# Layer 0's block attention with queries and outputs in seven block products each, beside each other in banks of their own and in a written-out order

## The chip, the cores and the metric

The kernel runs on one core of a Trainium2 chip. The time is device microseconds of one execution, the lower the better. TensorE is called PE here (its weight loads PEld), VectorE DVE, ScalarE ACT, GpSimd POOL, and SyncE, which issues the DMAs, SP.

## The reference, cut to what matters

Two decoder layers on x of 8 sequences by 112 tokens by 512 channels (896 tokens), all in float32. Each layer has a self-attention, a cross-attention to a context and a third block. In Layer 0 the third block is a decoder block of its own: a grouped-query attention with 32 query heads and 4 key-value heads of 128 channels, and then a mixture of 32 experts. The change is in that attention:

```python
h = _rmsnorm(hidden_states, ln1_w)
q = (h @ Wq).reshape(B, S, 32, 128)      # Wq: 512 x 4096
k = (h @ Wk).reshape(B, S, 4, 128)       # Wk, Wv: 512 x 512
v = (h @ Wv).reshape(B, S, 4, 128)
q, k = _rope(q, pos), _rope(k, pos)
k, v = jnp.repeat(k, 8, axis=2), jnp.repeat(v, 8, axis=2)
scores = jnp.einsum('bqhd,bkhd->bhqk', q, k) / jnp.sqrt(128.0)
scores = jnp.where(causal, scores, -1e9)
attn = jax.nn.softmax(scores, axis=-1)
o = jnp.einsum('bhqk,bkhd->bqhd', attn, v).reshape(B, S, 4096) @ Wo   # Wo: 4096 x 512
x = resid + o
```

The experts that follow read x, and the residual path needs the x from before as well.

## The kernel before

**Layout.** Activations stand either with tokens on partitions (x and y, seven tiles of 128 tokens by 512 channels) or transposed with channels on partitions (hT: four chunks of 128 channels by 896 tokens). HALF is 448 tokens, half of all. The eight PSUM banks of 128 x 512 float32 are named by hand: bank 0 and 1 for projections (`mm_ps`), 2 and 3 for scores (`sc_ps`), 4 and 5 for transposes (`tp_ps`), 6 and 7 for averages (`o_ps`), each pair used in turn.

**The attention** (`l0_block_attention`). The 32 query heads go in eight head groups, hg, of four heads; two groups share one key-value head. First come the keys of all heads and the queries of group 0 (`project_T`, 128 channels by 448 tokens at a time, four matmuls each; `rope_halves` turns each with one DVE multiplication, two DVE multiplications of 64 partitions and one POOL addition), then the values. Then, for each group, a loop over the eight sequences b; one turn of it is called a step here. A step holds:

- `probabilities`: four score matmuls of 112 x 112, on DVE the scale and mask, the row maximum and its subtraction, the exponential on ACT, on DVE the row sum and its reciprocal, on POOL the division;
- `project_queries`: one block of the next group's queries, 128 channels by 448 tokens (32 matmuls a group; an fp32 matmul is two PE records, so 64), and its rope;
- `average`, two steps late: four transposes of the probabilities, a copy to SBUF by ACT, one matmul with the values, a copy to oT by ACT;
- `project_out`, LAG = 5 tiles late: one tile of 128 tokens of oT times Wo's part of the group, four matmuls of 512 columns, and an addition to y by DVE;
- `gather_weights`: DMAs that bring one part of the experts' weights from one place in DRAM to another, which wait for a value of this step so that they are spread over the stage.

The weights of a group, wq and wo, are loaded into a pool of six tiles (`load_w`). The stage isn't ordered by hand: the framework's scheduler sets the order of the instructions on each engine by its own costs. Other stages put `with in_order():` around their work, which keeps each engine to the order in which the code issues.

**Seven products.** Layer 1's FFN already multiplies matrices in two by two blocks with seven block products where eight are usual, by `seven_products`. Sums and differences of blocks stand in for the blocks: `row_sums` makes four of the stationary side, `column_sums` four of the moving side. Partial results stay in three PSUM banks a, b, c: a collects a first product, is copied by ACT, collects the next on top, is copied again, and so on; `take` adds a copy to a bank and stores the block:

```python
product(a, top[0], left[0], first=True);  m1 = copied(0)
product(c, rows[0], columns[0], first=True)
product(a, rows[1], columns[1]);          u2 = copied(1)
product(b, top[1], left[1], first=True)
product(a, rows[2], columns[2]);          u3 = copied(2)
take(1, 1, c, u3);  take(0, 0, b, m1)
product(a, bottom[1], columns[3]);        take(1, 0, a, None)
product(c, rows[3], right[1]);            take(0, 1, c, u2)
```

In the trace before, L259 is the projections' matmul, L888 scores, L304 transposes, L913 averages, L841, L844 and L848 the rope, L904 the division, L306 and L917 ACT's copies, L922 the addition to y, L1410 the matmul of the seven products, L1387 to L1390 the row sums and L1394 to L1397 the column sums. L80 is the line of an engine wrapper, which every instruction inside `in_order` has.

Of the kernel before, what the change touches and what calls it, by code (L numbers as in the profile page):

```python
# [21 lines left out]
FP = mybir.dt.float32  # L22
# [36 lines left out]
def decoder(ctx: ExitStack, tc: tile.TileContext, a, out: bass.AP):  # L59
# [756 lines left out]

    def block_norm(y, t, root):

        mvr = row_scales(x[t], root, (ONCE, twice(1e-5)))
        yield  # L820
        xn = normed_rows()
        normed(xn, x[t], mvr, mvr[:, 3:4])
        shift = sm.tile([P, 1], FP, tag="shift", name="shift", bufs=8)
        V.tensor_scalar(shift, mvr[:, 0:1], mvr[:, 2:3], -1.0, ALU.mult, ALU.mult)
        A.activation(y[t], x[t], AF.Identity, bias=shift, scale=mvr[:, 2:3])
        return xn
# [23 lines left out]
    def l0_block_attention(y, hT, late, weights, prepare):  # L850
# [5 lines left out]

        wk_, wv = load_w(a["f0_wk"], "f0_wk"), load_w(a["f0_wv"], "f0_wv")
        with phase("f0", "tile") as p0:
            kT = p0.tile([P, 4, NT], FP, tag="kT", name="kT")
# [10 lines left out]
            v = p0.tile([S, B, D], FP, tag="v", name="v")  # L870
            for half in range(2):
                for g in range(4):
                    rope_halves(kT[:, g, half * HALF : (half + 1) * HALF], project_T(hT, wk_, g, half))
                for j in range(4):
                    project_queries(qT, wq, 4 * half + j)
                if half == 0:
                    for xn, t in late:
                        transpose_tile(hT, xn, t, ln1w)
            for b in range(B):
                pp = mm_ps()  # L880
                matmul_k(pp[:S, :], lambda k: hT[:, k, b * S : (b + 1) * S], lambda k: wv[:, k, :])
                A.copy(v[:, b, :], pp[:S, :])

            def probabilities(hg, qT, b):
                sc = sc_ps()
                tok = slice(b * S, (b + 1) * S)
                for j in range(4):
                    T.matmul(  # L888
                        sc[:S, j * S : (j + 1) * S], qT[:, j, tok], kT[:, hg // 2, tok],
                        start=True, stop=True,  # L890
                    )
                s = work[0].tile([S, 4, S], FP, tag="s", name="s", bufs=4)
                V.scalar_tensor_tensor(
                    s, sc[:S, : 4 * S].rearrange("p (j q) -> p j q", j=4),
                    128.0**-0.5, causal4, ALU.mult, ALU.add,
                )
                mx = sm.tile([S, 4], FP, tag="mx", name="mx")
                V.tensor_reduce(mx, s, AX.X, ALU.max)
                softmax_exp(s, mx)
                den = sm.tile([S, 4], FP, tag="den", name="den")  # L900
                V.tensor_reduce(den, s, AX.X, ALU.add)
# [3 lines left out]
                return s  # L905

            outs = o_ps()

            def average(hg, oT, b, s):
                pT = transpose_probs(s, "pT")  # L910
                po = outs[b % 2]
                kv = hg // 2
                T.matmul(  # L913
                    po[:, : 4 * S], v[:, b, kv * P : (kv + 1) * P],
                    pT.rearrange("p j q -> p (j q)"), start=True, stop=True,
                )
# [4 lines left out]
            def project_out(oT, wo, t):  # L921
                V.tensor_tensor(y[t], y[t], project_rows(oT, wo, t), ALU.add)  # L922

            halves = [a[n].rearrange("e p k n -> (e p) (k n)") for n in ("e0_wg", "e0_wu", "e0_wd")]

            def gather_weights(step, s):

                r = slice(step * P // 2, (step + 1) * P // 2)
                nc.sync.dma_start(weights[step * P // 2 : step * P // 2 + 1, :: KC * NI], s[:1, 0, :3])
                for i, src in enumerate(halves):  # L930
                    nc.sync.dma_start(weights[r, i * KC * NI : (i + 1) * KC * NI], src[r, :])

            waiting, finished = [], []
            for hg in range(8):
                wo = load_w(a["f0_wo"][hg], "f0_wo")
                oT = p0.tile([P, 4, NT], FP, tag="oT", name="oT", bufs=2)
                if hg < 7:
                    qT_next, wq = new_queries(hg + 1)
                else:
                    prepare()  # L940
                for b in range(B):
                    waiting.append((hg, oT, b, probabilities(hg, qT, b)))
                    gather_weights(hg * B + b, waiting[-1][3])
                    if hg < 7:
                        project_queries(qT_next, wq, b)
                    if len(waiting) > 2:
                        average(*waiting.pop(0))

                    if b < NTT:
                        finished.append((oT, wo, b))  # L950
                    if len(finished) > LAG:
                        project_out(*finished.pop(0))
                qT = qT_next
            for one in waiting:
                average(*one)
            for one in finished:
                project_out(*one)
# [424 lines left out]


    def row_sums(dst, top, bottom, eng):


        eng.tensor_tensor(dst(0), bottom[0], bottom[1], ALU.add)  # L1387
        eng.tensor_tensor(dst(1), dst(0), top[0], ALU.subtract)
        eng.tensor_tensor(dst(2), top[0], bottom[0], ALU.subtract)
        eng.tensor_tensor(dst(3), top[1], dst(1), ALU.subtract)  # L1390

    def column_sums(dst, left, right, eng):

        eng.tensor_tensor(dst(0), right[0], left[0], ALU.subtract)  # L1394
        eng.tensor_tensor(dst(1), right[1], dst(0), ALU.subtract)
# [753 lines left out]
```

## Time and profile before

| | |
|---|---|
| median of three runs | 2036.97 us (2033.36 to 2041.16) |
| the profiled execution | 2040.25 us, span 2038.4 us |
| granted PE clock, mean | 0.976 |
| PE busy | 1930.7 us, 95% |
| DVE, ACT, POOL busy | 956.7, 589.5, 723.2 us |
| mean DMA rate | 103 GB/s |

A group line of the profile reads: line, engine, operation, output and inputs by the program's names, shapes, count, then total busy time and the mean length of one in ns, then the idle time before them and what ended it. Lengths of matmuls overlap, since PE is pipelined, so the distance from one start to the next is what one costs.

### The profile page before, as it was taken

To read this page: it belongs to the slowest core of one execution; us is meant where nothing else is said; L and a number is where in the kernel's file an instruction comes from. 1 tells how busy PE (TensorE), PEld (TensorE's weight loads), DVE (VectorE), ACT (ScalarE), POOL (GpSimd) and SP (SyncE) were. 2 spreads that over 40 slices of the span, in tenths; PEclk is the share of its full clock that TensorE was granted. 3 is DMA by queue.
4 is the path that set the end of the run, shared out by engine and by line. 5 is a ranking of instruction groups with operands and counts; after the bars stand their busy time and mean duration, and the time that the engine had idled before them with its cause. 6 is when DMAs were issued, how large, how long until landed. Compare 5 with 4: busy or idle time off the path is not lost. (4 is left out here: it accounts for less than half of the span.)

```text
span 2038.4 us, 26870 instructions
## 1 busy us (share of the span) xinstructions
PE 1930.7 (95%) x10113; PEld 1187.9 (58%) x10113; DVE 956.7 (47%) x1983; ACT 589.5 (29%) x1373; POOL 723.2 (35%) x875
## 2 busy tenths in 40 slices
PE   8999998999999999998999999989889898899999
PEld 4545664455555555554778888864555544445568
DVE  4662556375666656645222222214686556522260
ACT  3543321121122212232111111112466636422200
POOL 2253041132222222221456666631354302344371
PEclk9999989999999999989999999999999999999999
DMA  4105010143344343544886776754001120211100
GB/s 177 42 22 173 13 42 32 57 134 129 126 138 138 131 129 104 161 180 156 268 235 128 214 160 152 187 100 125 22 22 34 54 60 22 84 42 42 41 6 31
DMA packets 82024, 209.65 MB, mean 103 GB/s; under 512 B 32979, under 2 KB 38227, under 8 KB 72788
## 3 DMA queue, kind: packets, MB, share of 16 engines
q1 hardware_dynamic: 57588, 134.27, 20.0%
q0 software_dynamic: 24288, 73.47, 14.2%
q8 instruction: 86, 1.41, 0.3%
q14 instruction: 62, 0.51, 0.1%
HBM read 245.31 MB, written 78.76 MB: 159 GB/s over the span
## 5 line engine op out<-in xcount | busy, mean ns | idle before, releaser
L259 PE MATMUL bank<-f_wo,oT 128*128 128x512 f32 x448 | 210.5, 594 | 0.0
L259 PE MATMUL bank<-hT,f_wq 128*128 128x448 f32 x512 | 202.6, 540 | 0.0
L80 PEld LDWEIGHTS bank<-hbT,wb 128*128 128x128 f32 x1408 | 164.2, 192 | 20.6 <-issue 20.6
L904 POOL TENSOR_TENSOR s<-s,rec 112x448 f32<-112x448 f32 x64 | 59.8, 934 | 322.1 <-ACT pT L306 252.2
L80 DVE TENSOR_TENSOR hidb<-sgb,bank 128x256 f32<-128x256 f32 x66 | 27.8, 422 | 291.1 <-ACT sgb L80 229.4
L80 PE MATMUL bank<-hbT,wb 128*128 128x128 f32 x1408 | 164.3, 275 | 0.0
L259 PEld LDWEIGHTS bank<-hT,f_wq 128*128 128x128 f32 x512 | 93.8, 190 | 78.2 <-issue 77.8
L80 POOL TENSOR_TENSOR st<-st,rec 112x448 f32<-112x448 f32 (+1 forms) x95 | 82.9, 904 | 147.7 <-DVE rec L80 83.4
L259 PEld LDWEIGHTS bank<-f_wo,oT 128*128 128x128 f32 x448 | 80.7, 190 | 76.0 <-issue 76.0
L80 POOL DMA_INDIRECT acc<-ob,row_out x66 | 106.3, 1611 | 35.0 <-issue 18.3
L80 ACT ACTIVATE st<-st,mxs 112x112 f32<-112x112 f32 (+1 forms) x383 | 111.0, 379 | 0.0
L298 ACT ACTIVATE s<-s 112x448 f32<-112x448 f32 x64 | 36.9, 577 | 244.0 <-DVE s L297 234.3
L922 DVE TENSOR_TENSOR y<-y,bank 128x512 f32<-128x512 f32 x56 | 38.5, 688 | 124.6 <-PE bank L259 124.6
L848 POOL TENSOR_TENSOR qT<-qT,qs 128x448 f32<-128x448 f32 x64 | 72.4, 1132 | 63.3 <-DVE qs L844 63.3
L844 DVE TENSOR_TENSOR qs<-bank,shape_consts 64x448 f32<-64x448 f32 x144 | 89.5, 622 | 2.9
L80 PE MATMUL bank<-wb,hidb 128*128 128x512 f32 x176 | 84.5, 603 | 0.0
L80 ACT ACTIVATE sgb<-bank 128x256 f32<-128x256 f32 x66 | 25.4, 384 | 202.6 <-PE bank L80 179.0
L80 POOL DMA_INDIRECT hrow<-hrows,row_in x66 | 63.9, 969 | 47.0 <-DVE free L80 23.2
L80 POOL DMA_INDIRECT wb<-weights,wrow x44 | 46.3, 1052 | 95.9 <-PE bank L80 74.1
L1410 PE MATMUL bank<-tok,sums 128*128 128x448 f32 x192 | 78.1, 541 | 2.0 <-DVE tok L1394 1.4
L80 ACT ACTIVATE ob<-bank,pw 128x512 f32<-128x512 f32 x66 | 45.4, 688 | 118.8 <-PE bank L80 117.3
L888 PEld LDWEIGHTS bank<-kT,qT 128*112 128x112 f32 x512 | 59.6, 178 | 27.6 <-issue 25.6
(407 smaller groups left out, 3680.9 us busy)
## 6 DMA issues: line engine op xcount, KB each, us to landing
weights<-in_e_wg SPq DMA_DIRECT2D x64, 256.0 KB
weights<-in_e_wu SPq DMA_DIRECT2D x64, 256.0 KB
weights<-in_e_wd SPq DMA_DIRECT2D x64, 256.0 KB
f_wq<-in_f_wq SPq DMA_DIRECT2D x8, 1024.0 KB
f_wo<-in_f_wo SPq DMA_DIRECT2D x8, 1024.0 KB
cTe<-in_ctxT SPq DMA_DIRECT2D x8, 558.0 KB
f_wg<-in_f_wg SPq DMA_DIRECT2D x4, 1024.0 KB
f_wu<-in_f_wu SPq DMA_DIRECT2D x4, 1024.0 KB
```

The costliest lines, as they stand in the source:

```text
L80: done = issue(*args, **kw)
L259: T.matmul(dst, lhs(k), rhs(k), start=(k == 0), stop=(k == n - 1))
L298: A.activation(s, s, AF.Exp)
L844: V.tensor_tensor(qs[lo : lo + 64], src[hi : hi + 64], sin0[lo : lo + 64].unsqueeze(1).to_broadcast([64, HB, S]), ALU.mult,)
L848: G.tensor_tensor(d, d, qs, ALU.add)
L888: T.matmul(sc[:S, j * S : (j + 1) * S], qT[:, j, tok], kT[:, hg // 2, tok], start=True, stop=True,)
L904: G.tensor_tensor(s, s, rec.unsqueeze(2).to_broadcast([S, 4, S]), ALU.mult)
L922: V.tensor_tensor(y[t], y[t], project_rows(oT, wo, t), ALU.add)
L1410: T.matmul(dst, lhs(k), rhs(k), start=first and k == 0, stop=k == terms - 1, skip_group_check=True)
```

## The change

Queries of groups 1 to 7 and outputs of all groups become seven block products.

- Queries: two products p a group, each two heads by both halves of the tokens, `row_sums` of wq on POOL for each (`qsum`). The token side is summed once for all groups: one sum takes the place of half of hT, three stand in the tiles of x, so x is written to DRAM first (`far_x`) and read back at the end.
- Outputs: tiles of tokens in three pairs, each two tiles by two halves of 256 output channels; `row_sums` of oT on POOL (`osums`), four sums of wo a group on DVE (`osum`). The seventh tile is done as before (`last_output`). Blocks are added to y by DVE from PSUM and by POOL from a copy.
- Banks: bank 5 for scores, bank 6 for transposes and averages, (0, 4, 1) and (7, 4, 1) as a, b, c for queries, (2, 4, 3) for outputs.
- Only two key heads and value heads stay in SBUF; the other two go to DRAM (`far_k`, `far_v`) and come back in groups 2 and 4.
- Softmax: negated scores and a minimum, four exponentials a step on ACT with the minimum as a bias, each of which sums its row itself, for one exponential with a subtraction and a sum on DVE. The division comes one step later. `gather_weights` waits for the row sums.
- The whole stage is `in_order`. Pieces of the products are generators, one piece a block product, in two lists (0: queries, 1: outputs); `fill` runs three times in a step, after the scores, between transposes and average, and after the average, and takes pieces from both lists up to a share of what the group wants. A piece's `row_sums` are issued when it is among the first two of its list and its inputs are there.
- `row_sums`, `column_sums`, `seven_products` and helpers move up in the file; `seven_products` yields after every block product. Layer 1's FFN calls the same functions and keeps its order.

The diff, cut to its core:

```diff
+        product(a, top[0], left[0], first=True)
+        m1 = copied(0)
+        yield
+        product(c, rows[0], columns[0], first=True)
+        yield
+        product(a, rows[1], columns[1])
+        u2 = copied(1)
+        yield
...
+        if terms < 4:
+            take(0, 0, b, m1)
+        yield
...
-            for half in range(2):
-                for g in range(4):
-                    rope_halves(kT[:, g, half * HALF : (half + 1) * HALF], project_T(hT, wk_, g, half))
-                for j in range(4):
-                    project_queries(qT, wq, 4 * half + j)
+            for t in range(NTT):
+                nc.sync.dma_start(far_x[t * P : (t + 1) * P, :], x[t])
+            for g in (3, 2, 1, 0):
+                kT = new_keys()
+                for half in range(2):
+                    rope_halves(kT[:, half * HALF : (half + 1) * HALF], project_T(hT, wk_, g, half))
+                if g < 2:
+                    keys[g] = kT
+                else:
+                    nc.sync.dma_start(far_k[g - 2], kT)
+                project_queries(qT, wq, 7 - g)
...
+            product_banks = [(bank[0], bank[4], bank[1]), (bank[2], bank[4], bank[3]),
+                             (bank[7], bank[4], bank[1])]
+
+            def query_products(qT, wq, p):
+                top, bottom = blocks_of(wq, p)
+                sums = p0.tile([P, 4, 2, P], FP, tag="qsum", name="qsum", bufs=2)
+                row_sums(lambda i: sums[:, i], top, bottom, G)
+                yield
+                copies = [normed_rows()[:, :HALF] for _ in range(3)]
+
+                def take(m, half, pp, more):
+                    if more is not None:
+                        V.tensor_tensor(more, pp, more, ALU.add)
+                        pp = more
+                    later.append((qT[:, 2 * p + m, half * HALF : (half + 1) * HALF], pp))
...
+            def output_products(oT, wo, columns, p, which=1):
...
+                row_sums(lambda i: sums[:, i], top, bottom, G)
+                yield
...
+                def take(m, n, pp, more):
+                    d = y[2 * p + m][:, n * NI : (n + 1) * NI]
+                    V.tensor_tensor(d, d, pp, ALU.add)
+                    if more is not None:
+                        G.tensor_tensor(d, d, more, ALU.add)
...
+            def exps(s, mn):
                 den = sm.tile([S, 4], FP, tag="den", name="den")
-                V.tensor_reduce(den, s, AX.X, ALU.add)
+                for j in range(4):
+                    A.activation(s[:, j, :], s[:, j, :], AF.Exp, bias=mn[:, j : j + 1], scale=-1.0,
+                                 accum_out=den[:, j : j + 1])
+                return s, den
...
+            def fill(share):
+
+                for _ in range(2):
+                    for which in range(2):
+                        if given[which] < share * wanted[which]:
+                            go_on(which)
+                if later:
+                    rope_halves(*later.pop(0))
+
+            waiting, undivided, rest = [], [], None
+            with in_order():
+                for hg in range(8):
...
+                    done = hg * B
+                    given[:] = 0, 0
+                    wanted[:] = 16 * (hg < 7), 25 if hg else 9
+                    if rest:
+                        add(1, output_products(*rest, 1), done - 3)
+                    if hg < 7:
+                        for p in range(2):
+                            add(0, query_products(qT_next, wq, p))
+                    else:
+                        wanted[:] = 16, 13
...
+                    for b in range(B):
...
+                        scores(hg, qT, b)
+                        fill((3 * b + 1) / (3 * B))
+                        s, mn = find_minima()
+                        waiting.append((hg, oT, b, s))
+                        if undivided:
+                            divide(*undivided.pop())
+                        one = waiting.pop(0) if len(waiting) > 2 else None
+                        if one:
+                            pT = turned(one[3])
+                        fill((3 * b + 2) / (3 * B))
+                        if one:
+                            average(*one[:3], pT)
+                            averaged[0] += 1
+                            make_ready()
+                        if b == 4:
+                            columns = output_sums(wo)
+                        if b == 5:
+                            add(int(hg < 7), output_products(oT, wo, columns, 0, int(hg < 7)), done + 3)
+                        undivided.append(exps(s, mn))
+                        gather_weights(hg * B + b, undivided[0][1])
+                        fill((3 * b + 3) / (3 * B))
...
+                divide(*undivided.pop())
+                for one in waiting:
+                    go_on(0)
+                    go_on(1)
+                    average(*one[:3], turned(one[3]))
...
+            for t in range(NTT):
+                nc.sync.dma_start(x[t], far_x[t * P : (t + 1) * P, :])
```

## The prediction

> **What bounds the kernel now.** I read the page first (busy times and the forty slices), then the busy time by stretch, then PE in order of time inside the stage, then the groups by line and shape.
>
> ```profile
> PE 1930.7 (95%) x10113; PEld 1187.9 (58%) x10113; DVE 956.7 (47%) x1983; ACT 589.5 (29%) x1373; POOL 723.2 (35%) x875
> PE   8999998999999999998999999989889898899999
> ```
>
> TensorE bounds the program as a whole. Layer 0's block attention lies in slices 9 to 18. By the view in order of time it runs from the first queries of head group 1 at 406.7 us to the first router transposes at 897.8 us, 491.1 us; PE is busy for 489.65 us of them, at clock 1.00. One head group (8 steps) of it:
>
> ```profile
> core 0: us, PE busy (x) PEld busy (x) DVE busy (x) ACT busy (x) POOL busy (x), PEclk, DMA share, GB/s
> 535.40:599.60 64.20, 64.20 (x233) 34.30 (x232) 39.56 (x71) 13.15 (x24) 16.51 (x16) 1.00 0.40 131
> ```
>
> Nothing waits here but the other engines: DVE has 25 us spare, ACT 51, POOL 48. So PE work taken out shows in full, unless the new order makes PE wait. One step of PE, repeated every 8.47 us:
>
> ```profile
> start us, us, engine line op out<-in xcount [idle before <-releaser]
> 600.60 0.55 PE L304 MATMUL bank<-ident,s 112*112 112x112 f32 x4
> 600.98 1.04 PE L259 MATMUL bank<-f_wo,oT 128*128 128x512 f32 x2
> 601.86 0.98 PE L913 MATMUL bank<-pT,v 112*128 112x448 f32 x2
> 602.68 2.74 PE L259 MATMUL bank<-f_wo,oT 128*128 128x512 f32 x6
> 605.25 0.95 PE L888 MATMUL bank<-kT,qT 128*112 128x112 f32 x8
> 606.04 3.19 PE L259 MATMUL bank<-hT,f_wq 128*128 128x448 f32 x8
> ```
>
> From start to start: transposes 0.38 us, average 0.82, scores 0.78, queries 3.02 (0.378 a record), outputs 0.43 a record. An fp32 matmul is two records. Seven steps in eight have outputs, so a group should take 8 x 8.47 - 3.44 = 64.3 us, as measured.
>
> **What comes off PE.** Queries of groups 1 to 7: 64 records of 448 columns become 56. Layer 1's FFN already runs seven products with such matmuls, one each 0.376 us (eight `tok,sums` records take 3.01 us start to start), so 64 x 0.378 - 56 x 0.376 = 3.1 us a group, 21.9 us in seven. Outputs of all eight groups: 56 records of 512 columns (24.0 us) become 84 of 256 plus 8 of 512 for the last tile. The rows of 256 columns are in Layer 1's FFN too, where 32 records go from 1965.22 to 1972.13, 0.216 us each: 84 x 0.216 + 8 x 0.43 = 21.5, 2.5 us less a group, 19.9 in eight. Together 41.8 us. A group keeps 58.5 us of PE.
>
> **What the other engines get.** The rows:
>
> ```profile
> L80 ACT ACTIVATE st<-st,mxs 112x112 f32<-112x112 f32 x203 | 59.5, 384 | 0.0
> L1389 POOL TENSOR_TENSOR sums<-f_wg 128x256 f32<-128x256 f32 x8 | 6.2, 779 | 0.0
> L2022 DVE TENSOR_TENSOR x<-x,bank 128x256 f32<-128x256 f32 x12 | 5.0, 421 | 55.0 <-POOL x L2021 34.2 <-PE bank L1410 20.8
> L1394 DVE TENSOR_TENSOR colsum<-f_wd 128x512 f32<-128x512 f32 x4 | 2.6, 685 | 1.3 <-issue 1.3
> L1397 DVE TENSOR_TENSOR colsum<-f_wd,colsum 128x512 f32<-128x512 f32 x4 | 11.3, 2834 | 0.0
> ```
>
> ACT: 32 exponentials at 0.38 plus 0.19 to read each sum (the read-accumulator row of L965), 16 copies of PSUM at 0.53, 6 query copies at 0.53, 9 output copies at 0.37: 33 us a group. DVE loses the subtraction and the sum of the softmax (16 x 0.63) and gains 6 query additions at 0.62, 4 weight sums at 0.69 and 12 additions at 0.42 for 7 at 0.69: about 39 us. POOL gets 20 sums and 9 additions of 256 columns at 0.78 on top of 8 ropes (1.13) and 8 divisions (0.93): 39 us. All fit under 58.5, so none costs anything by its amount. What costs is the fixed order.
>
> **What the order costs.** I walked the order of the changed program against these durations, with about 0.2 us from an engine's end to the next one's start (pT's copy starts 0.25 after the transposes end).
>
> Between transposes and average PE must fill 0.85 us (copy 0.53 and two hand-overs). One output product (four records, 0.86) just does, so an ordinary step costs nothing. If that cover fails, as at 424.03 before the stream is full, it costs 0.89 (the row says so); bank 6, now alone for both, adds 0.75 after the average, which outputs and the next scores cover.
>
> At the head of a group POOL has to make four sums for outputs and then eight for queries, all of them queued behind its last output addition of the group before. The second query product needs the fifth of these sums. After the last product of the old group ends: 0.2, DVE's addition 0.42, 0.2, POOL's addition 0.78, five sums of 0.75, 0.1: 5.5 us. PE gets there after scores, two products, transposes: 3.5. PE waits 2.0; if DVE is late with the reciprocal that POOL's division ahead of these needs, up to 3.4. I take 2.3 for groups 2 to 6 (nearer to the direct chain), 1.1 and 0.4 for groups 1 and 7: 13.0 us, bounds 3 and 20. The division of the step queues behind the burst too (11.9 us after), but is wanted only at 13.
>
> Group 0: token sums on DVE before the second product and before the score bank is free (1.4), first output sums (2.0), an output product too soon after its copy (0.7), a last step with nothing between transposes and average (0.9): 5.0, bounds 3 and 8. The same short gap costs 0.25 in later groups and ACT's exponentials fill 80% of the short steps of group 7: 3.0, bounds 0 and 6.
>
> Tail: the last three transposes and averages have nothing between them, and the last exponentials (four of 0.57) stand on ACT ahead of the next pT copy: 10.3 us for 3.6 of PE work, and 0.8 for two products that share bank 4. 7.5, bounds 4 and 9.
>
> Moved and hidden: rearranged first projections and the later finish of y's tiles, 1.0 (minus 2 to 4; today's PE wait before the third key block is 2.0). Twenty-eight more DMAs on SP (x, keys and values out and back, 0.33 to 0.8 us each to issue) beside 32 issues a group, with the engines at a DMA share of 0.41: nothing. Each query weight stands behind two or three steps' weight copies but is issued 12 us or more before use; late, it would hold POOL's sums and PE at the head of a group, up to 5 us. The copies now start from the denominators, earlier than from the divided scores, and queue nothing new.
>
> Lastly DVE beside POOL: a sum of two SBUF operands took 0.685 us alone and 2.83 while POOL ran sums of about that length. Ropes from copies and the weight sums are of this kind, 22 a group. DVE's slack takes it at half a POOL instruction (0.4 us) each; I put 1.5 us on the path, bounds 0 and the first rival below. The Trainium skill, "SBUF — State Buffer", section "Who interferes with whom", says that a DVE instruction with two SBUF inputs and a GpSimd instruction that reads SBUF block each other for the whole instruction, which these two rows bear out. It speaks against this change; by it alone the sum stays as it is where such an instruction waits for what is left of one of POOL's, and loses its gain where each waits for a whole one.
>
> Sum: 5.0 + 13.0 + 3.0 + 7.5 + 1.0 + 1.5 = 31.0, less today's own waits there (0.9 at 424, 0.6 in the tail) = 29.5. Gain 41.8 - 29.5 = 12.3 us. The profiled execution took 2040.25 us (span 2038.4), 3.3 above the median of the runs; 2027.95 less 3.3 gives 2024.7, say 2025. With all lower bounds the costs are 8 less 1.5 and the gain is 35; with all upper ones, the port left at 1.5, they are 48.5 less 1.5, a loss of 5.
>
> **Rivals.** (1) Slower: the port shared by DVE and POOL. If each of the 22 instructions waits for a whole POOL instruction (mean 39 / 45 = 0.87 us), DVE needs 39 + 19 = 58 us, as much as PE, and as it must still wait for PE about 1.1 us in each step, a group takes 67: 2.7 more than now, 16 in groups 1 to 6. With the rest (15 lost at the two ends by the terms above, 8 saved on PE in groups 0 and 7) that is 23 more, 2060. It decides once more than 2 us a group reaches PE beyond my sum. For it: the 2.83 us. Against: POOL is idle a third of the time, and most additions read PSUM (0.42 and 0.62 beside a busy POOL in Layer 1). (2) The stream holds: POOL clears the sums before PE asks, or the wait absorbs others. Costs 3 + 3 + 1.5 + 7.5 less 1.5, gain 28: 2009. Against: the last output addition stands ahead of the sums. (3) All is eaten: heads at 20 and 0.1 us in each of 62 steps at bank 6 leave nothing: 2038. That 256-column products save nothing is excluded by 0.216.
>
> **How the numbers follow.** My forecast 0.40 (gain 4 to 20), rival 2 0.27, rival 3 0.18, rival 1 0.15. About 0.5%, 10 us, is what a measurement can tell from no change: seven tenths of the forecast and all of rival 2 lie beyond: faster 0.28 + 0.27 = 0.55; same 0.12 + 0.18 = 0.30; slower 0.15. Range: 2006 (gain 31) to 2044 (loss 7, just past the upper bounds), which leaves out nearly all of rival 1 and the best of rival 2, 2 in 10.
>
> **What would show it.** Right: 232 more PE records (56 fewer for queries, 288 more of half the length for outputs), PE busy about 448 us of some 479 in this stage; in PE's waits POOL's `qsum`, some 2 us once a group, and ACT's pT in the tail. Wrong: DVE instructions with `xn` or `f_wo` inputs well over 0.9 us, PE waiting for ACT's `oc`, `xn` or pT in each step, or query weights landing late.

## The result, and the profile after

The changed kernel takes 2045.49 us (median of 20 runs, 2040.74 to 2054.07); the kernel before, run beside it, 2035.72 (median of 20). The ratio is 1.0045 with a 95% interval of 1.0033 to 1.0058: some 9 us slower, where 12 us faster was forecast. The profiled execution took 2048.99 us (span 2047.1), 3.5 above that median.

From the page of the changed kernel:

```profile
PE 1913.2 (93%) x10345; PEld 1246.4 (61%) x10345; DVE 962.7 (47%) x1993; ACT 691.3 (34%) x1939; POOL 890.2 (43%) x1099
PE   8989999989999999979999999998989898899999
PEclk9999989999999999978999999999999999999999
```

The 232 additional PE records are there (10345 against 10113), but PE's busy time fell by 17.5 us, not by 42, and the dent in the clock at the end of the block attention, which the kernel before had in slice 18 alone (0.8), is two slices wide (18 and 19, 0.7 and 0.8).

The busy times by stretch: the first group, a middle group, and the stretch from the last output product to the experts' first product (the router's, 71.10 us at clock 0.86 before).

```profile
core 0: us, PE busy (x) PEld busy (x) DVE busy (x) ACT busy (x) POOL busy (x), PEclk, DMA share, GB/s
403.26:455.64 52.38, 43.98 (x185) 27.20 (x183) 36.22 (x64) 22.95 (x80) 20.00 (x21) 0.97 0.37 133
517.77:579.80 62.03, 59.29 (x261) 40.09 (x260) 40.49 (x71) 26.90 (x96) 38.47 (x46) 1.00 0.49 161
897.20:977.75 80.55, 68.06 (x248) 41.68 (x248) 41.66 (x119) 22.31 (x43) 20.82 (x28) 0.77 0.45 160
```

The last of these before the change:

```profile
897.80:968.90 71.10, 61.05 (x248) 36.57 (x247) 37.47 (x110) 15.95 (x24) 16.63 (x25) 0.86 0.44 159
```

Where the time went, by milestones of the two profiled executions: the values are projected at 403.26 instead of 406.74 (3.5 gained); the attention takes 493.9 us instead of 491.1 (2.9 lost, 12 were to be gained); the router's stretch takes 80.55 instead of 71.10 (9.5 lost). Together 8.9; the executions differ by 8.7. A middle group does get shorter, 62.03 us against 64.3, but only by 2.3. Its head and its end, in PE's order of time:

```profile
520.93 0.55 PE L80 MATMUL bank<-ident,s 112*112 112x112 f32 x4
522.78 1.77 PE L80 MATMUL bank<-hT,qsum 128*128 128x448 f32 x4 [1.30 <-POOL qsum L80]
...
576.79 0.92 PE L80 MATMUL bank<-pT,v 112*128 112x448 f32 x2
578.84 1.13 PE L80 MATMUL bank<-f_wo,osums 128*128 128x256 f32 x4 [1.13 <-DVE y L80]
579.80 0.95 PE L80 MATMUL bank<-kT,qT 128*112 128x112 f32 x8
```

The first wait was forecast, at 2.3 us; the second was not. A wait costs more than its bracket: transposes take 0.385 us from start to the next start when nothing waits, here 1.85, so a bracket of 1.30 costs 1.47, and 0.09 more until the products run at full rate. In what follows "lost" is counted so: the time from one start to the next, less what the same records take undisturbed (0.385 the transposes, 0.755 an average, 0.785 the scores, 0.38 a record of a query, 0.216 and 0.43 of an output). By this count PE's work in the attention fell from 486.2 to 445.2 us, by 41.0, and what it lost rose from 4.9 to 48.8.

The end of the attention, PE in order of time, and then the first of ACT's squares for the norms that follow:

```profile
877.90 1.86 PE L80 MATMUL bank<-pT,v 112*128 112x448 f32 x2 [0.68 <-ACT pT L80]
879.56 3.17 PE L80 MATMUL bank<-f_wo,oT 128*128 128x256 f32 x8
882.56 3.62 PE L80 MATMUL bank<-osum,osums 128*128 128x256 f32 x16
...
893.70 3.60 PE L80 MATMUL bank<-f_wo,oT 128*128 128x512 f32 x8
901.78 0.66 PE L235 MATMUL bank<-ident,xn 128*128 128x128 f32 x4 [4.48 <-DVE xn L1242]
```

```profile
898.06 0.60 ACT L1239 ACTIVATE bank<-y 128x512 f32<-128x512 f32 x1 [7.24 <-DVE y L80]
```

After four short waits (0.68 to 1.24 us, from 870 on) PE runs at half speed: the average at 877.90 takes 1.86 us where an undisturbed one takes 0.92, eight output records take 3.00 us (879.56 to 882.56); the next sixteen, at full speed again, take 3.46. And ACT stands idle for 7.24 us before the first square, though two of the seven y tiles were finished at 870; before, the norms of the first tiles were made between the tail's products and the first transposes followed the last product without a wait.

### The profile page after: what moved, and what is told of

Its sections match the earlier page's. It is cut to its first block, busy times and chain, and to the rows that moved or that the text cites. A ratio compares the mean times of both kernels' runs of the same rounds, so it can differ in the third digit from the quotient of the medians.

```text
span 2047.1 us, 28256 instructions
## 1 busy us (share of the span) xinstructions
PE 1913.2 (93%) x10345; PEld 1246.4 (61%) x10345; DVE 962.7 (47%) x1993; ACT 691.3 (34%) x1939; POOL 890.2 (43%) x1099
## 5 line engine op out<-in xcount | busy, mean ns | idle before, releaser
L80 POOL TENSOR_TENSOR qT<-qT,qs 128x448 f32<-128x448 f32 x56 | 63.5, 1133 | 112.0 <-DVE qs L80 112.0
L80 ACT COPY pT<-bank 112x448 f32<-112x448 f32 x128 | 66.7, 532 | 100.7 <-PE bank L80 99.5
L80 ACT ACTIVATE s<-s,mn 112x112 f32<-112x112 f32 x256 | 96.1, 379 | 6.5 <-DVE rec L80 6.4
L80 DVE TENSOR_TENSOR y<-y,bank 128x256 f32<-128x256 f32 (+1 forms) x104 | 43.8, 434 | 112.2 <-PE bank L80 111.2
L80 PE MATMUL bank<-f_wo,oT 128*128 128x256 f32 (+1 forms) x256 | 83.2, 441 | 1.9 <-DVE y L80 1.9
L80 POOL TENSOR_TENSOR s<-s,rec 112x448 f32<-112x448 f32 x64 | 62.1, 970 | 49.5 <-DVE rec L80 49.5
L80 PE MATMUL bank<-osum,osums 128*128 128x256 f32 x288 | 72.9, 381 | 4.1 <-POOL osums L80 4.1
L80 ACT COPY oT<-bank 128x448 f32<-128x448 f32 x80 | 42.4, 530 | 85.4 <-PE bank L80 85.4
L80 PEld LDWEIGHTS bank<-f_wo,oT 128*128 128x128 f32 x256 | 48.6, 194 | 34.6 <-issue 23.2
```

The lines of the kernel that those rows point to most:

```text
L80: done = issue(*args, **kw)
```

## Experiments

Theory after this reading: the seven products give PE what was forecast, and four local things take it away: DVE in group 0, a queue on POOL at each group's head, DVE late at each group's end, and norms that cannot begin beside the tail. The rivals name for each another engine that would only move the wait, or the half clock as the common cause. Each kernel below is the changed kernel with the edit shown, timed beside the kernel before; the ratios are to that kernel, so a ratio is to be held against 1.0045.

**Squares in other banks.**

```
-            sq = sc_ps()
+            sq = bank[6 + t % 2]
```

> The seven squares of the norms before the router are written to banks 6 and 7 instead of 2 and 3; nothing else is edited. In the changed kernel the first of them starts at 898.06 us, after the addition of the last output tile (897.34), although the first y tiles were done at 870. Theory (banks): the squares stand behind the output products because those occupy banks 2 and 3. Then tiles 0 and 1 are normed inside the tail, the 4.48 us wait of PE before the first transposes goes, PE stays warmer, and the stretch from the last output to the experts' first products falls from 80.6 to 72 to 75 us; the kernel takes 2038 us (2036 to 2041), about 1.001 of the kernel before. Rival (half clock): what is lost there is the slow clock that the waits of the tail leave behind (0.77 granted in this stretch against 0.86 before); then the stretch stays above 78 us and the time at 2043 to 2046. Rival (sequence): ACT takes a square only with a table load between the tail's copies, and the tail grows by what the router saves: 2045.

2037.56 us, 1.0004 (0.9992 to 1.0017). The first square now runs inside the tail, and the router's stretch takes 70.91 us:

```profile
881.05 0.60 ACT L1239 ACTIVATE bank<-y 128x512 f32<-128x512 f32 x1
```

```profile
897.97:968.88 70.91, 59.69 (x249) 35.76 (x248) 38.75 (x115) 17.99 (x33) 17.69 (x26) 0.88 0.57 205
```

The theory of the banks holds. `sc_ps` gives banks 2 and 3, and the change made these the output products' own until the last one; the squares, which only want a place to write, waited for them. The last group and the tail took 1.4 us more in this run, much less than the router's stretch gave back. The clock follows (0.88 against 0.77): it was not carried over from the tail, for in the changed kernel it was full again between the two, and fell anew after PE's wait of 4.48 us:

```profile
875.30:882.13 6.83, 5.44 (x14) 3.51 (x14) 0.00 (x0) 1.97 (x4) 5.59 (x9) 0.50 1.00 360
882.20:897.20 15.00, 14.48 (x59) 10.68 (x57) 3.19 (x8) 1.86 (x5) 4.35 (x6) 1.00 0.58 203
902.61:929.92 27.31, 25.28 (x92) 20.27 (x93) 13.84 (x46) 6.15 (x14) 8.13 (x7) 0.50 0.47 173
```

If the clock is either full or half, as here, the means of 0.77, 0.86 and 0.88 stand for an estimated 37 us of the stretch at half clock in the changed kernel, 20 before and 17 in this run: at half clock half of each us is lost, so that most of the 9.5 us went there. How much the stretch loses varies between executions: in six other runs that do not touch it (scores read first, third bank early, query sums first, and the first three with one part alone) it took 75.8 to 79.2 us, so 80.55 is on the high side.

**The scores read first.**

```
                         scores(hg, qT, b)
-                        fill((3 * b + 1) / (3 * B))
                         s, mn = find_minima()
+                        fill((3 * b + 1) / (3 * B))
```

> In every step the two DVE instructions that read the score bank are issued ahead of the step's first products and their rope, instead of behind them. Theory (score bank): with one bank for scores, PE waits in group 0 and at its end for DVE to read it (1.92 at 424.30 and 2.12 at 455.64), because a rope of 2.9 us stands ahead on DVE, and after both waits the next 12 records run at half speed (1.8 and 1.6 us lost). All of it goes: 4.5 of waits and 3.4 of slow records, 7 to 8 us off: 2038 us (2036 to 2040), with group 0 at 46 us instead of 52.4. Rival (DVE's amount): in group 0 DVE has ropes for 36 of 52 us and PE would meet the same backlog one product later, at a bank whose rope is not done or at ACT's copies; then under 2 us come off: 2043.5 to 2045.5. In groups 2 to 6, where PE never waits for the score bank, both expect nothing (62.0 us).

2041.72 us, 1.0032 (1.0014 to 1.005): 4 us better by the medians, though the intervals overlap, and group 0 takes 51.45 us, not 46. PE's waits in group 0:

```profile
425.51 0.59 PE L80 MATMUL bank<-ident,s 112*112 112x112 f32 x4 [1.86 <-POOL s L80]
...
453.68 1.05 PE L80 MATMUL bank<-kT,qT 128*112 128x112 f32 x8 [1.89 <-DVE s L80]
```

The theory of the score bank falls, the rival of DVE's amount stands, though the time lies between the two forecasts: the wait of 1.92 for `s` became one of 1.86 for the division, whose reciprocal now stands behind the same rope. DVE is never idle here from 411 to 426.

**The third bank added early.**

```
         product(c, rows[0], columns[0], first=True)
+        if early:
+            take(1, 1, c, None)
...
-        take(1, 1, c, u3)
+        take(1, 1, None if early else c, u3)
```

> The addition of an output product's third bank to y is issued as soon as its first product is made (second piece), not with the sixth piece; its other addend follows on POOL as before. Theory (DVE late at the end of a group): PE's wait for DVE's y, 1.13 us before the last output product of each group, 1.5 us with the drain and refill of the array, goes at 7 group ends: 10 us off, 2035.5 us (2034 to 2038), groups 2 to 6 at 60.5 us. Rival (POOL decides the head): at the end of a group POOL stands behind its division (578.62) and two additions to y, which wait for DVE's reciprocal and not for PE, so the twelve sums for the next group start only 0.3 us sooner; PE arrives 1.5 earlier and waits 1.2 longer for the query sums (2.5 instead of 1.30): groups at 61.7, 2 to 3 us off, 2043 us.

2062.72 us, 1.0132 (1.0108 to 1.0157): 17 us slower than the changed kernel. The wait for y is gone from the group ends (one of 0.80 us for DVE's `s` stands there now), but groups 2 to 6 take 64.9 us:

```profile
585.30 0.55 PE L80 MATMUL bank<-ident,s 112*112 112x112 f32 x4
588.75 3.35 PE L80 MATMUL bank<-hT,qsum 128*128 128x448 f32 x4 [2.90 <-POOL qsum L80]
```

The rival was right about the mechanism and wrong about the size: PE waits 2.90 us where it waited 1.30, and then runs four query records at half speed (3.15 us instead of 1.52). A wait moved to another place is not free of its length: two of about a microsecond left the clock alone, this one did not.

**Query sums first at a group's head.**

```
+                    if hg < 7:
+                        add(0, query_products(qT_next, wq, 0))
                     if rest:
                         add(1, output_products(*rest, 1), done - 3)
                     if hg < 7:
-                        for p in range(2):
-                            add(0, query_products(qT_next, wq, p))
+                        add(0, query_products(qT_next, wq, 1))
```

> At the head of a group POOL makes the four sums for the first query products ahead of the four for the outputs, instead of behind them. Theory (queue on POOL): the sums that PE waits for (1.30 us, 1.56 with drain and refill, at the head of groups 2 to 6) come 2.9 us sooner, the wait goes, and the output sums, wanted 1.6 us after, come just in time: 8 us off, 2037.5 us (2036 to 2040), groups at 60.5. Rival (the wait moves): the output sums are now 2.9 us later and PE stops at the second output product instead, for 1 us or more: groups at 61.7 to 62, 2043.5 to 2045.5 us.

2037.70 us, 1.0000 (0.9984 to 1.0015). PE's wait for `qsum` is gone from its waits, and a middle group takes 60.54 us, 1.5 less:

```profile
582.07:642.61 60.54, 59.10 (x261) 39.95 (x260) 41.00 (x71) 26.90 (x96) 38.46 (x46) 1.00 0.41 137
```

The theory of POOL's queue holds: the order in which twelve sums stand there was worth the whole wait.

**Products in the holes of the tail.**

```
                 divide(*undivided.pop())
+                add(1, output_products(*rest, 1))
                 for one in waiting:
                     go_on(0)
                     go_on(1)
-                    average(*one[:3], turned(one[3]))
+                    pT = turned(one[3])
+                    go_on(1)
+                    go_on(1)
+                    average(*one[:3], pT)
...
+                    go_on(1)
-                add(1, output_products(*rest, 1))
```

> In the tail the seven products of the third and fourth output tiles, which need none of the last two averages, are put between the last transposes and averages instead of behind them. Theory (waits and the clock): from the last scores (868.92) to the first output product of the tail (879.56) PE has 10.6 us for 2.9 of work, and the 34 records after it run at half speed and lose 2.7 more. With products in the holes 5 to 8 us come off: 2039 us (2037 to 2041), last group and tail 62 to 64 us instead of 69.2. Rival (other engines): the four sums of these products follow two divisions on POOL and ACT's copies of the products stand ahead of its pT copies, so PE waits for osums and pT as long as before: last group and tail 67 or more, 2043 to 2045.5.

2037.72 us, 1.0006 (0.9991 to 1.0020), the time of the theory, but not by its way: last group and tail take 69.42 us, as long as before the edit (69.2). The rival names the reason:

```profile
873.77 3.78 PE L80 MATMUL bank<-osum,osums 128*128 128x256 f32 x8 [2.87 <-POOL osums L80]
```

The sums stood behind the last division on POOL, which waits for the last exponentials, and after 2.87 us PE was at half speed again (eight records in 3.57 us). The gain is in the router's stretch (71.45 us): the last product in bank 2 now ends earlier in the tail, and the first square starts 2.9 us before the end of the last product instead of 0.9 after it. Once more the bank.

**One part alone.** Queries or outputs go back to whole products, in the fixed order. For the queries:

```
+                    pp = bank[(0, 1, 7)[(4 * p + i) % 3]][:, :HALF]
+                    for k in range(KC):
+                        T.matmul(pp, wq[:, k, (2 * p + m) * P : (2 * p + m + 1) * P],
+                                 hT[:, k, half * HALF : (half + 1) * HALF], ...)
+                        if k == KC - 1: later.append((qT[...], pp))
+                        if k % 2: yield
```

and for the outputs:

```
+                    pp = bank[((0, 1), (3, 2))[which][t % 2]]
+                    for k in range(KC):
+                        T.matmul(pp, oT[:, k, t * P : (t + 1) * P], wo[:, k, :], ...)
+                        if k == KC - 1: V.tensor_tensor(y[t], y[t], pp, ALU.add)
+                        yield
```

> The fixed order, the banks, the softmax and the parked keys, values and x of the changed kernel, but queries and outputs as whole products (eight, as in the kernel before), so with no sums, no copies and no additions beside y's. Theory (the sums and additions cost the groups, the order costs both ends): groups 1 to 6 take 64.3 to 64.6 us, as before the change; group 0 loses 2 to 4 us, the tail 6 to 8, the router's stretch stays at 76 to 80 us; the first projections gain 3.5: 2049 us (2045 to 2053), ratio 1.005 to 1.008. Rival (the order costs every step): one bank for scores and one for transposes and averages cost 0.2 us or more in every step whatever the products are: groups of 66 or more, group 0 as late as in the changed kernel (12 us lost): 2062 us.

> Queries in seven products as in the changed kernel, outputs as whole products of 512 columns. Theory: POOL then has no output sums and no additions to y ahead of the query sums and PE has no wait at a group's head, nor for DVE's y at its end: groups of 61.3 to 61.6 us (64.3 less 3.06); group 0 still loses about 10 us, because DVE's additions and ropes from copies fall into its short steps; tail and router as in the changed kernel: 2040 us (2036 to 2043). Rival (the head wait comes from the sums' own amount): PE still waits for qsum and groups take 62.5 or more: 2048 us.

> Outputs in seven products as in the changed kernel, queries as whole products whose ropes read PSUM. Theory (ropes from copies make DVE late at the end of a group): with ropes of 1.9 us from PSUM in the place of additions and ropes of 3 us and more, PE's wait for DVE's y goes, groups take 61.8 to 62.4 us (64.3 less 2.5 and small gaps), group 0 loses 5: 2038 us (2034 to 2042). Rival (the bank decides): the third bank is read late whatever the ropes cost, the wait of 1.5 stays at 7 group ends and groups take 63.3 to 64: 2047 us.

In the first and the third of these runs the whole query products read tokens that the sums had overwritten in part; the attention runs through the same instructions, but the tokens are routed otherwise and what follows the router's stretch takes some 45 us more (2093.25 and 2087.80 us in all), so these two are read up to the router only. The queries alone take 2030.21 us, 0.9968 (0.9949 to 0.9986), below the expected 2036 to 2043. Group 0 and a middle group, of the order alone and then of the queries alone:

```profile
400.47:445.66 45.19, 44.51 (x181) 25.91 (x180) 26.85 (x51) 18.23 (x70) 14.49 (x14) 1.00 0.46 154
...
573.14:636.88 63.74, 63.74 (x233) 34.86 (x232) 29.77 (x55) 20.45 (x81) 16.55 (x17) 1.00 0.43 139
```

```profile
404.19:452.74 48.55, 44.10 (x174) 24.97 (x172) 31.88 (x58) 21.97 (x77) 14.18 (x14) 0.96 0.42 143
...
576.15:637.00 60.85, 60.85 (x226) 33.19 (x225) 34.57 (x62) 23.75 (x86) 22.52 (x25) 1.00 0.45 146
```

The order alone loses 0.9 us in group 0 and nothing in a middle group, which is 0.6 shorter than before the change (0.5 of it in the eight averages, 0.755 us each to the next start instead of 0.82). So the rival of a cost in every step falls: what the order costs is the tail (last group and tail 69.6 us) and the router's stretch (77.0). The queries alone save 2.89 us a group (3.06 forecast) and nothing waits, but they lose 7.3 us in group 0. The outputs alone take 62.09 us a group, 1.65 saved of 2.5, with small gaps and a short wait for `osums` (0.27), and lose 8.2 us in group 0. Were the parts additive, both would take 63.74 - 2.89 - 1.65 = 59.2; together they take 62.03. These 2.8 us are about the two waits, 1.56 at the head and 1.39 at the end: neither exists with one part alone.

> The fixed order with whole products for queries and outputs again, without the sums of tokens that overwrote half of the normed tokens in the first such run (its routing differed, so that only its times up to the router could be read). Left out: those eight DVE sums. Theory, from that run's stages (attention 497.2 us against 491.1, router 77 against 71.1, first projections 3.5 shorter): 2044 us (2041 to 2048). Rival (the sums delay the start of the stage): 2040 us.

2041.47 us, 1.0033 (1.0015 to 1.005): the order by itself costs some 5 us. The interval holds both the theory's 2044 and the rival's 2040, so the two stay undecided. The profiled execution, at 2035.04 well below that median, has a router's stretch of 72.6 us.

**The repairs together.** Four edits, with the third and fourth output tiles' sums put ahead of the last division:

```
+                add(1, output_products(*rest, 1))
                 divide(*undivided.pop())
-                add(1, output_products(*rest, 1))
```

> The changed kernel with four edits together: squares in banks 6 and 7, DVE's reads of the scores ahead of the step's products, the first query sums ahead of the output sums at a group's head, and the third and fourth output tiles in the holes of the tail, with their sums on POOL ahead of the last division instead of behind it. Theory (separate causes): 8 us for the squares, 8 for the order of the sums, 3 for the scores and 3 to 5 for a shorter tail (last group and tail 65 us) come off 2045.5: 2022 us (2018 to 2027), groups of 60.3 to 60.5 us. Rival (shared cause, the half clock or an engine behind): squares and tail repair the same stretch and count once, the rest does not add: 2030 us or more.

> The four edits and the early addition of an output product's third bank, which alone made the kernel 17 us slower because PE came sooner to the query sums and waited 2.9 us for them at half speed after. Theory (chain of the head): with the query sums first on POOL that wait has 2.9 us of cover, so the early addition now takes away PE's wait for DVE's y without a new one: groups of 58.8 to 59.2 us, 9 us less than the four edits: 2013 us (2009 to 2019). Rival (POOL is late in any case, by its division and additions at the end of the group): PE meets the query sums 1.5 us sooner and waits again: groups of 60.3 or more, 2022 us or more.

2025.62 us, 0.9946 (0.9928 to 0.9963), and 2019.49 us, 0.9922 (0.9903 to 0.9941). With four, groups take 60.34 us, and last group and tail 63.3 instead of 69.2: the tail's holes fill once the sums are made in time. The time lies in the theory's range, but the four gains taken singly (8, 4, 8 and 8 us) would make some 27, not the 20 reached: the squares and the filled tail shorten the same stretch, the router's, which takes 72 us with both and 71 with either. The fifth brings nothing in the attention (478.6 us against 479.1): groups stay at 60.4, because PE, no longer held up at the end, waits at the head:

```profile
581.29 1.99 PE L80 MATMUL bank<-osum,osums 128*128 128x256 f32 x8 [1.07 <-POOL osums L80]
```

By its groups the rival is right again. The time lies between the two forecasts: of the 5 us between the two profiled executions all but 0.4 lie outside the attention (1.7 in the router's stretch), and no run shows their cause.

> The five repairs, and the last addition of each rope inside the head groups moved from POOL (1.13 us, 8 a group) to DVE (about 0.62). Theory (POOL late by its own work): POOL loses 9 us a group, two of these additions at the end of a group; its sums start 1.1 to 2.2 us sooner, PE's wait for the output sums (1.07, 1.4 with drain and refill) goes: groups of 58.6 to 59.2, 2011 us (2007 to 2016). Rival (DVE late): the last scores of a group are read by DVE at 573.90 behind two ropes, 4 us after PE made them, and POOL's division and additions wait for that; with 5 us more a group on DVE they come 1.2 us later still: groups of 60.4 to 62, 2020 to 2030 us.

```
-                    rope_halves(*later.pop(0))
+                    rope_halves(*later.pop(0), V)
```

2029.48 us, 0.9970 (0.9949 to 0.9990), slower than the five repairs it starts from, with groups of 61.33. POOL's busy time fell from 38.3 to 29.4 us a group, and PE's wait for `osums` stayed at 1.08 while one of 0.54 for DVE's `s` was added. DVE's busy time rose from 39.7 to 43.1. So POOL is late less by its own work than by DVE: its division waits for the reciprocal, which stands behind ropes and the scores' minima. In the changed kernel, DVE in order of time at a group's end:

```profile
574.07 1.30 DVE L80 TENSOR_TENSOR qT<-xn,shape_consts 128x448 f32<-128x448 f32 x1
575.39 1.69 DVE L80 TENSOR_TENSOR qs<-xn,shape_consts 64x448 f32<-64x448 f32 x2
577.11 0.62 DVE L80 SCALAR_TENSOR_TENSOR s<-bank,causal 112x448 f32<-112x448 f32 x1
...
578.39 0.72 DVE L80 TENSOR_TENSOR y<-y,bank 128x256 f32<-128x256 f32 x2
```

PE began the scores at 573.53; DVE reads them at 577.11, after a rope, and comes to y at 578.39, just before PE goes on.

**Each half, repaired.** Queries in seven products with whole outputs, and the reverse, each with the squares, the scores read first and the filled tail (the reverse also with the early addition).

> Queries in seven products, outputs as whole products, with squares in banks 6 and 7, DVE's reads of the scores first, and output products in the holes of the tail. Theory: groups stay at 60.8 us (nothing waits there), the squares and the tail bring 10 to 13 us and group 0 one: 2018 us (2014 to 2023) against 2030.2. Rival (the tail's outputs cannot start sooner, PE waits for ACT's pT as before): 2024 us.

> Outputs in seven products, queries as whole products, with the squares, the scores read first, the early addition and the filled tail; the eight DVE sums of tokens, which nothing needs here, are left out. Theory (each half pays alone): whole products for queries leave DVE with ropes of 1.9 us from PSUM and POOL with no query sums, so a group takes 61.3 to 61.6 us (63.74 for whole products alone, less 2.5 and the gaps), group 0 about 45: 2020 us (2015 to 2025), slower than the queries' half repaired (2009.6) and about as fast as both halves together (2019.5). Rival (output sums wait in any company): groups stay at 62 or more and the time at 2027 or more.

2009.61 us, 0.9881 (0.9851 to 0.9911), the fastest of all, faster than both kernels and than its own expectation (2014 to 2023); and 2034.78 us, 0.9984 (0.9963 to 1.0005). Of the queries, repaired: group 0, a middle group, the router's stretch:

```profile
400.79:446.99 46.20, 42.36 (x174) 24.24 (x172) 31.16 (x58) 21.56 (x77) 14.02 (x14) 1.00 0.45 151
568.73:629.57 60.84, 60.84 (x225) 33.18 (x225) 35.13 (x62) 23.75 (x86) 22.36 (x25) 1.00 0.45 146
873.80:935.29 61.49, 52.84 (x248) 30.43 (x247) 38.44 (x111) 16.73 (x27) 16.75 (x25) 0.97 0.54 193
```

No group after the first loses anything, group 0 is 6.2 us shorter than in the changed kernel, and the router's stretch 19, 9.6 shorter even than before the change, with the clock at 0.97 there. Whole products finish y tile by tile, with no additions on POOL behind them; but the kernel before did so too, at 0.86; why the clock held here no run shows. The outputs' half keeps groups of 62.1 and a group 0 of 51.6 us (its rival's case; I had the gaps too small). Beside repaired queries, outputs in seven products save 0.4 us a group, and cost 3.6 in group 0, 3.2 in the tail and 8.9 in the router's stretch.

One control is missing: whole products in the fixed order with the same repairs. Of the 35 us between the profiled executions of the kernel before and of the repaired queries, 18 lie in the attention, 10 in the router's stretch and 6 ahead of the attention, and the order and the repairs may have a share in each. What the queries' seven products give without repairs is some 11 us, from 2041.47 (the order alone) to 2030.21.

## Why the prediction was wrong, step by step

By its own terms, profiled execution against profiled execution:

| term of the sum | forecast, us | measured, us |
|---|---|---|
| PE work taken out | -41.8 | -41.0 |
| group 0 | 5.0 | 12.0 |
| heads of groups 1 to 7 | 13.0 | 9.7 |
| group ends, PE waits for DVE's y | none | 8.3 |
| short gaps and group 7 | 3.0 | 8.6 |
| half clock at the start of group 1 | none | 1.6 |
| tail | 7.5 | 8.6 |
| lost in the kernel before | -1.5 | -4.9 |
| first projections and router | 1.0 | 6.0 |
| port of DVE and POOL | 1.5 | within the above |
| sum | -12.3 | +8.9 |

**What comes off PE** was right to 1 us, and so were its rows: 2.89 a group for the queries, and the outputs' records at 0.216. Of the 4.9 lost before, most is the averages, which took 0.82 us there and 0.755 after; this gain was not in the sum.

**Moved and hidden** is the step that failed worst as reasoning. It put "the later finish of y's tiles" and the projections at 1.0 together. The projections gained 3.5, the router's stretch lost 9.5. I had followed data and not banks: I costed the tiles' later finish, and never asked where the squares are written. Their banks, changed in one line, were worth 8 us.

**Group 0** was costed wait by wait at 5.0 and lost 12.0 (brackets of 8.4, what they cost beyond the brackets, and half-speed records of 1.8 us at 424). Its steps have no outputs yet, so they are short, about 5 us, and DVE's additions and ropes from copies fall into them. I had checked DVE's amount against a whole group ("39 under 58.5") and not against this one. The runs with one part alone show it in part: 0.9 us lost with whole products, 7.3 with the queries' sums. But the outputs alone, whose ropes read PSUM, lose 8.2 there, by one wait for POOL's first output sums and the slow records after it:

```profile
436.67 2.08 PE L80 MATMUL bank<-osum,osums 128*128 128x256 f32 x4 [3.81 <-POOL osums L80]
```

These sums were in the forecast at 2.0. With both parts it is 12.

**The heads** were seen, with the right cause, and a little too dear (1.56 instead of 2.3 in groups 2 to 6; the rest of the 9.7 is PE's waits for `osums` in group 7). **The group ends** were missed: DVE was taken to have slack because it has 21 us a group to spare, but in one fixed order a rope of 1.9 us and one of 3.0 stand ahead of the addition that frees the third bank (shown above, under the ropes on DVE). That "none costs anything by its amount" was true; the order was walked for POOL at the heads and not for DVE at the ends. **The short gaps** cost 0.8 us a group where 0.25 was taken, and group 7 3.6.

**The tail** was nearly right in size. Of what was to show it, the 232 records, one wait for `qsum` a group and pT in the tail came; PE busy came as 462 us of 494, not 448 of 479.

**The port** (the first rival) did not become the bound: DVE is busy 40.5 of 62 us, not 58. (The terms listed for DVE add up to 37, not to the 39 forecast.) But it is there. Ropes from copies, by form, in the changed kernel and in the one with the ropes' additions taken off POOL:

```profile
L80 DVE TENSOR_TENSOR qT<-xn,shape_consts 128x448 f32<-128x448 f32 x36 | 33.7, 936 | 0.6
```

```profile
L80 DVE TENSOR_TENSOR qT<-xn,shape_consts 128x448 f32<-128x448 f32 x36 | 23.5, 653 | 0.2
```

The same multiplication from PSUM takes 0.62 in both. The Trainium skill, "SBUF — State Buffer", section "Who interferes with whom", has a DVE instruction with two SBUF inputs and a GpSimd instruction that reads SBUF lock each other out; the rows agree in kind (0.94 beside a busy POOL, 0.65 beside a quieter one). In the changed kernel by itself, 24 of the 36 began while POOL was at work and took 0.83 to 1.31 us, the other 12 took 0.62. At the end of a group shown above, a rope's multiplications take 2.99 us instead of 1.87, and this 1.12 is as long as PE's wait for y; that the one causes the other no run showed.

Of the rivals, the third came nearest, "all is eaten" at 2038, though the 8 us beyond it went elsewhere than to heads and bank 6. Where the prediction went wrong as a whole was in the bounds: the terms not on the list (group ends, the squares' banks) had no bound at all.

## What to carry to other kernels

When a change takes PSUM banks or buffers for itself, list everyone else who writes there, later stages too, and not only those who need its data. Check an engine's slack against the shortest stretch and against its place in a fixed order, not against the mean of a group. When two halves of a change share queues, build each alone: here one half, repaired, is 1.2% faster than the kernel before, and adding the other half, repaired too, gives a third of that back.

## What the hardware showed that I had not expected

PE's half speed, a granted clock of 0.50 in the rows above, came after shorter and more scattered waits than I had reckoned with. After a single wait of 2.90 us (3.45 from the transposes' start to the next product's) four query records took 3.15 us instead of 1.52; after one of 1.30 they did not slow down. But in the tail no wait was longer than 1.24 us, and four of them (3.3 us together) within 6.5 us, with 2.3 us of work, were enough; in group 0 a wait of 1.92 was followed by slow records while one of 2.30 was not. The Trainium skill, "TensorE: Matmul & The Clock Gate", Part 1, ties the half clock to an idle window of about 3.4 us; the tail shows that no gap needs to be that long. A price for it belongs beside every wait of more than a microsecond or two: here 1.6 to 3.0 us after each place where the clock fell.
